# The steps ahead of the first routed tiles of a two-layer gated cross-attention kernel: moved between engines, cut into small steps and put in a written list

## The chip, the cores and the metric

The kernel runs on one core of a Trainium2 chip, as one launch. The time is that of the device in microseconds, the median of several runs. The core's engines work side by side, each through its own queue of instructions in order: TensorE (PE: matmuls into PSUM), VectorE (DVE), ScalarE (ACT), GpSimd (POOL), and SyncE (SP), which issues most of the transfers; GpSimd issues those with indices. They wait for each other through semaphores. A profile is one execution recorded by the hardware.

## The reference

Everything is float32; 4 batches of 512 tokens, 512 wide, so 2048 tokens in 16 tiles of 128. Two layers, each a gated attention and a gated mixture of experts:

```python
x = x + tanh(g_xattn[0]) * set_attention(layernorm(x), ctx, desc_router, W_q, b_q, itok)
x = x + tanh(g_ffn[0])   * moe32(layernorm(x), ...)     # 32 experts of 256, 6 per token, at most 192 tokens each, and a shared one
x = x + tanh(g_xattn[1]) * causal_mha(layernorm(x), ctx, ctx)
x = x + tanh(g_ffn[1])   * moe8(layernorm(x), ...)      # 8 experts of 352, 2 per token, and a shared one of 704
```

The parts that the change touches are those before the first layer's experts:

```python
# set_attention: 64 sets, each token allows 4 of them (itok), the best 2 are mixed
scores = einsum(layernorm(x) @ W_q.T + b_q, desc_router) / sqrt(512)
scores = where(mask, scores, -inf); top 2; softmax over the two
out = weights @ ctx                                   # per batch, 64 x 512
# moe32's router
scores = sqrt(softplus(h @ gate_w.T)); top 6 of scores + bias
weights = scores of the 6, divided by their sum, times 1.5
pos = running count of the expert's tokens in token order; kept if pos < 192
```

## The kernel before

The x of all 16 tiles stays in SBUF (`xs`). Tile t belongs to batch t // 4; group g (`GROUPS[g]`) is the tiles g, g+4, g+8, g+12, one of each batch. `lnT[g]` holds a group transposed (512 features by 512 tokens); at the start it is the plain x, loaded transposed, later the normalised one.

Up to the first routed tile (`before`, L270 to L711) the orders of TensorE, VectorE and ScalarE are as the program writes them (`manual_schedule`); GpSimd's and SyncE's are left to the scheduler. The work there:

- **Masks** (L293 to L301): for each of the 4 token blocks, VectorE compares the 64 set numbers with the 4 allowed ones (16 instructions), and makes the bias `bm`.
- **Scores' matrix** (L304 to L334): descT times W_q, its mean taken out (`msum`, `mrow`), transposed (`pmt`, `mT`). ScalarE and VectorE each have a part in it, in their queues behind the masks.
- **look1(u)** (L348): mean and variance of x of a part, by two VectorE instructions for a tile. The parts are group 0, group 1, and groups 2 and 3 together.
- **score1(p)** (L357): scores of two groups at once (`pss`), copied by ScalarE and transposed back (`pst`).
- **pick1(u)** (L372): the variance's rsqrt by arithmetic on VectorE (`rsqrt`), scaled and masked scores, the best two (`top_picks`), an exponential by a polynomial on VectorE (`exp_parts`), the weights `wa`.
- **mix1(u)** (L407): the weights transposed (`pw`, `wT`), times ctx; VectorE adds to x with the row sum, ScalarE squares for the next variance.
- **norm2, turn2(p)** (L458, L465): rsqrt, then eight normalised rows `h` on VectorE, each stored to `h_dram` and transposed into `lnT` (TensorE, copied by ScalarE).
- **logits2, gate2(p)** (L476, L502): router scores; gate2 is five steps, almost all on VectorE over 128x256 elements: an exponential, a log, a square root, the six best, the weights.
- **shared0(g, ..., early)** (L570): the shared expert of groups 0 and 1, as work for TensorE beside it.
- **counts** (L649 to L708): running counts of each expert's tokens (`rows2`, `upto`), totals `ptot`, counts `pcnt` to `cnt_dram`, positions `ppos`; from them `look2`, which tells which row of counts to fetch for a slot, and the keys from which each token's six slots are sorted.

Then GpSimd gathers counts (`find0`) and rows (`get0`), and 48 routed tiles of 128 slots run, two matmul groups each (`up0`, `down0`), each result stored to `y_dram`.

Between the layers (L895 to L1381) generators are advanced one step at a time by the list `ORDER`: `s` sums one gathered row of experts' results into x (76 of them, GpSimd gathers `NYK` = 7 ahead; the tiles in the order `FIRST`, `FETCH[t]` rows for a tile), `e2`, `e3` the first layer's shared expert of groups 2 and 3, `n`, `t`, `l` norm, transposition and router scores of a group, `q`, `a` the second attention, `r` the routing, `d` the second layer's shared expert, `k` and `w` loads, `p` the plan of the routed tiles.

The driver of the first part is a hand-written sequence of calls, with generators run to their ends or by `next`.

Of the kernel before, what the change touches and what calls it, by code (L numbers as in the profile page):

```python
# [9 lines left out]
F32 = mybir.dt.float32  # L10
I32 = mybir.dt.int32
AF = mybir.ActivationFunctionType
ALU = mybir.AluOpType
# [4 lines left out]
P = 128  # L18
# [26 lines left out]

ORDER = """
e2 k e2 s e2*2 s*4 e2*2 s*4 e3 s k s e3 s e2 s e2 s*6 n2 e3*2 s*2 e3 s e3 n2*2 t2 s e3 n2*2 s e3 s t2*3 l2 s*8
d2 s*3 d2 l2*2 q s*2 d2 s d2 a0 s d2*2 s*2 a0 a1 s a0 d2*2 s*4 d2 a0*2 d2 s*2 a0 s k a1 s*7 n0*4 s t0*2 n0
t0*2 a1 l0 s l0 s*2 d0 l0 s r0 a1 s*3 d0 a1*2 n3 s r0 d0*2 s*2 d0 n3*3 s r0 n3 s d0 r0 s d0 t3 d0 t3 s*5 n1
t3*2 r0*4 n1 d0 n1*3 l3 t1*4 l3 l1*2 l3 d3 r0 l1 d0 r1 p r1*3 d3*2 r1 d3*3 r1*4 p d3 p*2 w d1 d3 w d1 p d3*2  # L50
d1*3 p*2 d1*4 p d1
# [25 lines left out]
def flamingo_gated(  # L77
# [217 lines left out]
    for g in range(TB):  # L295
        V.tensor_scalar(mask[:, g, :], iota_f, itok_f[:, g, 0:1], None, ALU.is_equal)
        for k in range(1, KSET):
            V.scalar_tensor_tensor(
                mask[:, g, :], iota_f, itok_f[:, g, k : k + 1], mask[:, g, :], ALU.is_equal, ALU.max
            )  # L300
# [44 lines left out]
    def tiles1(u):  # L345
        return [t for g in PARTS[u] for t in GROUPS[g]]

    def look1(u):  # L348

        n = len(tiles1(u))  # L350
        s6 = sm12.tile([P, n, 6], F32, name=f"s61_{u}", tag="s61")
        mv = stats1[u] = sm12.tile([P, n, 2], F32, name=f"mv1_{u}", tag=f"mv1_{u}")
        for j, t in enumerate(tiles1(u)):
            V.bn_stats(s6[:, j, :], xs[t])
            V.bn_aggr(mv[:, j, :], s6[:, j, :])

    def score1(p):  # L357

        pss = ps.tile([P, S], F32, name=f"pss{p}", tag="g")
        for c in range(DC):  # L360
            for a in range(2):
                PE.matmul(
                    pss[a * N : (a + 1) * N, :], lhsT=mT[:, c, :], rhs=lnT[2 * p + a][:, c, :],
                    start=(c == 0), stop=(c == DC - 1),
                )
        sT = work.tile([P, S], F32, name=f"sT{p}", tag="sg")
        A.copy(sT, pss)
        scores1[p] = ps_t.tile([P, B, 2 * N], F32, name=f"pst{p}", tag="pt")
        for k in range(B):
            PE.transpose(scores1[p][:, k, :], sT[:, k * P : (k + 1) * P], ident)  # L370

    def pick1(u):  # L372
# [3 lines left out]
        a = sm12.tile([P, 5, n], F32, name=f"a1_{u}", tag="a1", bufs=2)  # L376
        va, d, m, q, r = [a[:, j, :] for j in range(5)]
        V.tensor_scalar(va, stats1[u][:, :, 1], EPS, None, ALU.add)
# [15 lines left out]
        exp_parts(r, d, m, q)  # L394
# [7 lines left out]
        gates1[u] = d  # L402

# [3 lines left out]
    def mix1(u):  # L407
# [12 lines left out]
        A.copy(wT[:, :na], pw)  # L420

# [31 lines left out]
    def cols(t):  # L453

        g, j = PLACE[t]
        return lnT[g][:, :, j * P : (j + 1) * P]

    def norm2(p):  # L458
        nm, ss, va, nb, _ = [norms2[p][:, j, :] for j in range(5)]
        V.tensor_scalar(va, ss, 1.0 / D, EPS, ALU.mult, ALU.add)  # L460
        rs = rsqrt(va, NP, f"b{p}")
        V.tensor_tensor(nb, nm, rs, ALU.mult)
        norms2[p] = rs, nb

    def turn2(p):  # L465

        rs, nb = norms2[p]
        for j, t in enumerate(tiles2(p)):
            h = work.tile([P, D], F32, name=f"h{t}", tag="row", bufs=NROW)
            V.tensor_scalar(h, xs[t], rs[:, j : j + 1], nb[:, j : j + 1], ALU.mult, ALU.add)  # L470
            nc.sync.dma_start(out=h_dram[t * P : (t + 1) * P, :D], in_=h)
            transposed(cols(t), h, f"pth{t}")
# [3 lines left out]
    def logits2(p):  # L476
        pl = ps.tile([P, S], F32, name=f"pl{p}", tag="u")
        for c in range(DC):
            for a in range(2):
                PE.matmul(  # L480
                    pl[a * E0 : (a + 1) * E0, :], lhsT=gate0_sb[:, c, :], rhs=lnT[2 * p + a][:, c, :],
                    start=(c == 0), stop=(c == DC - 1),
                )
        lT = work.tile([P, S], F32, name=f"lT{p}", tag="sg")
# [5 lines left out]
        A.copy(lgs[p], plt.rearrange("p k e -> p (k e)"))  # L490

# [9 lines left out]
    def gate2(p):  # L501
# [49 lines left out]
        for a in range(2):  # L551
            nc.sync.dma_start(out=hd[:, :, 2 * p + a, D:], in_=wts[:, :, a, :])

# [15 lines left out]
    def shared0(g, wgu, wd, early):  # L569

        it = work.tile([P, I0 // P, S], F32, name=f"it0s_{g}", tag="it")
        for ic in range(I0 // P):
# [8 lines left out]
            if not early:  # L581
                yield
# [25 lines left out]

# [3 lines left out]

    ws0 = load_w0(0, wsgu0, wsd0)
    mix = [mix1(u) for u in range(len(PARTS))]
    score1(0)
    look1(0)
    run(pick1(0))
    look1(1)
    next(mix[0])
    next(mix[0])  # L620
    score1(1)
    run(pick1(1))
    look1(2)
    next(mix[1])
    next(mix[1])
    pick = pick1(2)
    next(pick)
    norm2(0)
    turn2(0)
    run(pick)  # L630
    logits2(0)
    for _ in range(2):
        next(mix[2])
        next(mix[2])
    route0, route1 = gate2(0), gate2(1)
    early0, early1 = [shared0(g, *ws0, True) for g in range(EARLY)]
    next(early0)
    next(route0)
    norm2(1)
    next(early0)  # L640
    turn2(1)
    run(route0)
    logits2(1)
    run(early0)
    next(early1)
    next(early1)
    for _ in range(4):
        next(route1)
# [6 lines left out]
    V.tensor_tensor(row_sum, rows2[:, :, 3, :], sel2[:, :, 3, :], ALU.add)  # L655
    for k in range(B):
        V.tensor_tensor(upto[:, k + 1, :], upto[:, k, :], row_sum[:, k, :], ALU.add)
    V.tensor_tensor(rows2, rows2, upto[:, :B, None, :].to_broadcast([P, B, TB, E0]), ALU.add)
    ptot = ps.tile([P, NT, E0], F32, name="ptot", tag="g")
    prior = rows2.rearrange("p k j e -> p (k j) e")  # L660
    PE.matmul(ptot[:, : NT - 1, :], lhsT=ones, rhs=prior[:, 1:, :], start=True, stop=True)
    PE.matmul(ptot[:, NT - 1, :], lhsT=ones, rhs=upto[:, B, :], start=True, stop=True)
    run(route1)
    pcnt = ps.tile([P, B, P], F32, name="pcnt", tag="u")
    for k in range(B):
        PE.matmul(pcnt[:, k, :], lhsT=sel2[:, k, :, :], rhs=tri1, start=True, stop=False)
        PE.matmul(pcnt[:, k, :], lhsT=rows2[:, k, :, :], rhs=ones, start=False, stop=True)
    counts = work.tile([P, B, P], F32, name="counts", tag="row", bufs=NROW)
    A.copy(counts, pcnt)
    nc.sync.dma_start(out=cnt_dram[: NT * E0, :].rearrange("(k p) t -> p k t", p=P), in_=counts)  # L670
    ppos = ps.tile([P, NT, E0], F32, name="ppos", tag="o")
    PE.matmul(ppos, lhsT=tri, rhs=sel2.rearrange("p k j e -> p (k j) e"), start=True, stop=False)
    PE.matmul(ppos, lhsT=ones, rhs=prior, start=False, stop=True)

    ended = flat[:, : NT * E0]
    in_tile = sm12.tile([P, 2, E0], F32, name="in_tile")
    for h in range(2):
        V.tensor_scalar(ended, ptot.rearrange("p t e -> p (t e)"), slot_no[:, 0, h : h + 1], None, ALU.is_le)
        V.tensor_reduce(in_tile[:, h, :], ended.rearrange("p (t e) -> p e t", e=E0), AX.X, ALU.add)
    lookf = sm12.tile([P, NQ, 3], F32, name="lookf")  # L680
    for r, h, s_, p_ in ((0, 0, 0, slice(0, P)), (2, 0, 1, slice(0, P)), (1, 1, 0, slice(0, HC)), (1, 1, 1, slice(HC, P))):
        V.scalar_tensor_tensor(
            lookf[p_, :, r], in_tile[p_, h, s_::2], float(E0), expert[p_, :, r], ALU.mult, ALU.add
        )
    look2 = const.tile([P, NT2], I32, name="look2")
    V.tensor_copy(look2, lookf.rearrange("p q r -> p (q r)"))
    tok2 = const.tile([P, NT2], F32, name="tok2")
    V.scalar_tensor_tensor(
        tok2, lookf.rearrange("p q r -> p (q r)"), float(P // E0), neg4e.rearrange("p q r -> p (q r)"),
        ALU.mult, ALU.add,  # L690
    )
# [7 lines left out]
    back_, zrow_ = [  # L699
        v.rearrange("p q s -> p (q s)")[:, None, :].to_broadcast([P, NT, E0]) for v in (back, zrow)  # L700
    ]
    V.scalar_tensor_tensor(key2, ppos, float(P), back_, ALU.is_ge, ALU.mult)
    V.tensor_tensor(key2, key2, ppos, ALU.subtract)
    V.scalar_tensor_tensor(
        kept2, ppos, float(CAP), sel2.rearrange("p k j e -> p (k j) e"), ALU.is_lt, ALU.mult
    )
    V.tensor_tensor(key2, key2, zrow_, ALU.add)
    V.tensor_tensor(key2, key2, kept2, ALU.mult)  # L708
    run(early1)
# [197 lines left out]
    FIRST = [6, 2, 14, 10, 3, 11, 15, 7, 0, 4, 8, 12, 5, 1, 9, 13]  # L907
# [468 lines left out]
    for what in ORDER.split():  # L1376
        what, _, n = what.partition("*")
        for _ in range(int(n or 1)):
            next(does[what])
    for steps in does.values():  # L1380
        assert next(steps, None) is None  # L1381
# [233 lines left out]
```

## Time and profile before

| | us |
|---|---|
| median of 3 runs (lowest, highest) | 1103.65 (1103.22, 1107.76) |
| the profiled execution | 1109.61 |
| its span, first to last instruction | 1107.9 |

Busy time of the engines by stage of the profiled execution, in us, and the clock granted to TensorE (1 is full):

| stage | from, to | PE | DVE | ACT | POOL | clock |
|---|---|---|---|---|---|---|
| first scores and picks | 0, 33 | 15.9 | 20.8 | 3.7 | 6.4 | 0.71 |
| second and third part | 33, 62 | 11.0 | 26.6 | 6.7 | 0 | 0.68 |
| rows, logits, first gating | 62, 110 | 44.8 | 42.1 | 21.6 | 4.3 | 0.93 |
| second gating, counts | 110, 156 | 38.1 | 36.3 | 7.9 | 12.7 | 0.93 |
| routed tiles | 156, 456 | 298.0 | 92.9 | 64.0 | 91.5 | 1.00 |
| between the layers | 456, 700 | 202.7 | 141.7 | 61.8 | 131.1 | 0.78 to 0.93 in its parts |
| routed tiles of layer 2 and the end | 700, 1108 | 396.7 | 105.8 | 45.3 | 130.3 | 0.98 to 1.00 |

How to read what follows: a row of a timeline gives start, duration, engine, line, operation, output<-input, shape and count; in brackets the idle time before it and what ended that. A row of the windows gives the stretch, its length, the busy time of PE, PE's weight loads, DVE, ACT and POOL (with counts), the granted clock, the DMA engines' share and GB/s.

### The profile page before, as it was taken

The numbers are of one execution on the slowest core, as the hardware profiler recorded it, in microseconds if no ns is written. First come the engines' busy times: TensorE is split into PE (matmuls) and PEld (weight loads), VectorE is DVE, ScalarE is ACT, GpSimd is POOL, SyncE is SP. The second block draws the span as 40 slices with busy tenths as digits, with TensorE's granted clock in tenths as the row PEclk, the third lists the DMA queues.
The fourth block names the chain that finished last, engine by engine and source line by source line (L and its number), as shares of the span: only waits on it lengthen the run. The fifth ranks groups of instructions, "written<-read, shape, count | busy, mean of one in ns | idle before, by whom it ended". The sixth has DMA issues, their size and how long they took to land. (4 is left out here: it accounts for less than half of the span.)

```text
span 1107.9 us, 11070 instructions
## 1 busy us (share of the span) xinstructions
PE 1007.1 (91%) x3334; PEld 492.9 (44%) x3334; DVE 466.1 (42%) x1244; ACT 210.9 (19%) x461; POOL 376.3 (34%) x413
## 2 busy tenths in 40 slices
PE   5479889999999999969779896999999998999998
PEld 2134444444444444424434443655555555544443
DVE  5989946322222232357787443122222222218111
ACT  1144121222222222123343200211111111110000
POOL 2001142234332222276552562445545454310000
PEclk7679999999999999989969798999999999999999
DMA  8522047688788787765563107527453744438111
GB/s 320 234 76 77 11 125 238 222 275 283 257 294 287 253 288 248 252 204 172 145 206 115 48 5 207 184 74 238 133 163 107 248 115 145 135 117 313 38 38 38
DMA packets 88477, 191.94 MB, mean 173 GB/s; under 512 B 24638, under 2 KB 42078, under 8 KB 82016
## 3 DMA queue, kind: packets, MB, share of 16 engines
q1 hardware_dynamic: 59808, 114.59, 29.3%
q0 software_dynamic: 28608, 76.63, 23.4%
q8 instruction: 27, 0.44, 0.2%
q14 instruction: 34, 0.28, 0.1%
HBM read 206.16 MB, written 35.57 MB: 218 GB/s over the span
## 5 line engine op out<-in xcount | busy, mean ns | idle before, releaser
L801 PE MATMUL gu<-wbuf,xbT 128*128 128x512 f32 (+1 forms) x512 | 174.0, 596 | 1.7 <-ACT xbT L257 0.8
L967 POOL DMA_INDIRECT yk<-y_dram,rows_of x76 | 84.1, 1107 | 89.1 <-DMA kb<-in_kblk_dram 34.7
L783 POOL DMA_INDIRECT xb<-h_dram,get x48 | 48.1, 1002 | 165.5 <-issue 97.3
L1436 PE MATMUL pgr<-wbuf,xrT 128*128 128x352 f32 x288 | 93.2, 467 | 7.4 <-DMA wbuf<-in_wgu_dram,wrow 6.7
L1456 PE MATMUL por<-wbuf,itr 128*128 128x512 f32 (+1 forms) x216 | 98.7, 592 | 0.0
L801 PEld LDWEIGHTS gu<-wbuf,xbT 128*128 128x128 f32 (+1 forms) x512 | 63.1, 163 | 78.7 <-issue 77.3
L808 DVE SCALAR_TENSOR_TENSOR sgb<-gu,xb,sgb 128x256 f32<-128x256 f32 (+1 forms) x64 | 30.9, 483 | 157.6 <-ACT sgb L806 131.8
L1439 DVE SCALAR_TENSOR_TENSOR sgr<-pur,slots,sgr 128x352 f32<-128x352 f32 x36 | 21.0, 584 | 170.0 <-PE pur L1436 105.1
L826 PE MATMUL pob<-wbuf,itb 128*128 128x512 f32 (+1 forms) x256 | 91.2, 599 | 0.0
L1436 PE MATMUL pur<-wbuf,xrT 128*128 128x352 f32 x288 | 91.1, 459 | 0.0
L1227 PE MATMUL pg<-lnT,wbuf 128*128 128x512 f32 (+1 forms) x224 | 85.3, 560 | 0.1
L1459 POOL DMA_INDIRECT y_dram<-yr,put x36 | 36.9, 1025 | 126.5 <-DVE yr L1458 113.6
L1227 PE MATMUL pu<-lnT,wbuf 128*128 128x512 f32 (+1 forms) x224 | 79.5, 531 | 0.0
L1436 PEld LDWEIGHTS pur<-wbuf,xrT 128*128 128x128 f32 x288 | 54.7, 190 | 30.5
L1436 PEld LDWEIGHTS pgr<-wbuf,xrT 128*128 128x128 f32 x288 | 52.7, 193 | 32.1 <-issue 4.5
L1243 PE MATMUL po<-wbuf,it 128*128 128x512 f32 x128 | 61.2, 612 | 3.0 <-DVE x L1253 3.0
L1456 PEld LDWEIGHTS por<-wbuf,itr 128*128 128x128 f32 (+1 forms) x216 | 41.0, 190 | 41.9 <-issue 34.9
L761 POOL DMA_INDIRECT found<-cnt_dram,look x48 | 48.7, 1014 | 25.9 <-issue 14.0
L1227 PEld LDWEIGHTS pg<-lnT,wbuf 128*128 128x128 f32 (+1 forms) x224 | 35.6, 183 | 43.8 <-issue 42.0
L1227 PEld LDWEIGHTS pu<-lnT,wbuf 128*128 128x128 f32 (+1 forms) x224 | 35.0, 175 | 40.8 <-issue 38.1
L831 DVE COPY y<-pob 128x512 f32<-128x512 f32 x48 | 33.2, 692 | 45.3 <-PE pob L826 32.0
L1458 DVE TENSOR_TENSOR yr<-por,half_db 128x512 f32<-128x512 f32 x36 | 24.9, 692 | 57.5 <-PE por L1456 51.2
(398 smaller groups left out, 1279.2 us busy)
## 6 DMA issues: line engine op xcount, KB each, us to landing
wbuf<-in_wgu_dram SPq DMA_DIRECT2D x32, 1024.0 KB
wbuf<-in_wd_dram SPq DMA_DIRECT2D x32, 512.0 KB
y_dram<-y SPq DMA_DIRECT2D x48, 256.0 KB
q<-rp SPq DMA_DIRECT2D x256, 32.0 KB
y<-y_dram SPq DMA_DIRECT2D x32, 256.0 KB
lnT<-in_xT_dram SPq DMA_DIRECT2D x4, 1024.0 KB
x<-in_x_dram SPq DMA_DIRECT2D x16, 256.0 KB
h_dram<-h SPq DMA_DIRECT2D x16, 256.0 KB
```

The source lines that it names most:

```text
L761: G.indirect_dma_start(out=found[k][:, j, :], out_offset=None, in_=cnt_dram[:, :], in_offset=bass.IndirectOffsetOnAxis(ap=look2[:, i : i + ...
L783: G.indirect_dma_start(out=rows0[i], out_offset=None, in_=h_dram[:, :], in_offset=bass.IndirectOffsetOnAxis(ap=get2[:, i : i + 1], axis=0) ...
L801: PE.matmul(gu[p_, :], lhsT=xbT[:, c, p_], rhs=weights[e][0][:, c, :], start=(c == 0), stop=(c == DC - 1),)
L808: V.scalar_tensor_tensor(sg[p_, :I0], gu[p_, I0:], xb[p_, D + e : D + e + 1], sg[p_, :I0], ALU.mult, ALU.mult)
L826: PE.matmul(po[p_, :], lhsT=it[:, ic, p_], rhs=weights[e][1][:, ic, :], start=(ic == 0), stop=(ic == I0 // P - 1),)
L831: V.tensor_copy(y, po)
L967: G.indirect_dma_start(out=yk, out_offset=None, in_=y_dram[:, :], in_offset=bass.IndirectOffsetOnAxis(ap=rows_of[:, t, k : k + 1], axis=0) ...
L1227: PE.matmul(p_[m, :n], lhsT=wgu[:, a, c, i], rhs=lnT[g][:, c, k], start=(c == 0), stop=(c == DC - 1))
L1243: PE.matmul(po, lhsT=it[:, ic, k * P : (k + 1) * P], rhs=wd[:, ic, :] if ic < 2 else wd2, start=(ic == 0), stop=(ic == 2),)
L1436: PE.matmul(p_, lhsT=xbT[:, c, :], rhs=wgu[:, a, c, :], start=(c == 0), stop=(c == DC - 1))
L1456: PE.matmul(po, lhsT=it[:ni, ic, :], rhs=wd[:ni, ic, :], start=(ic == 0), stop=(ic == 2))
L1459: d = G.indirect_dma_start(out=y4_dram[:, :], out_offset=bass.IndirectOffsetOnAxis(ap=put4[:, i : i + 1], axis=0), in_=yr, in_offset=None, ...
```

## The change

The masks are formed on GpSimd by differences and products, with one compare on VectorE. look1 takes the mean by matmuls of the transposed x with a column of ones, and the squared deviations by ScalarE. pick1's exponential is ScalarE's. The normalised rows `h` are ScalarE's, in a step of their own apart from the transposition. score1, pick1, mix1, norm2, logits2, gate2 and the early shared0 get more step ends (`yield`). The counts become a generator. A new helper `in_steps` advances generators by a list, and the first part is driven by `FIRST_ORDER`; `j` in it is a matmul whose result nobody reads. `ORDER` is another list of the same steps, and `FIRST` another order of the tiles within each group.

```diff
+FIRST_ORDER = """
+c0 c1 c0*2 c1 c0*2 b0*2 f0 c1 f0*2 c1*2 f1 m0*3 f1 j c2*2 b1 f1 c2 m1*2 b1 c2*3 m1 c2*2 n0 c2 h0*4 t0 h0 t0 h0
+f2 t0 f2*2 t0*2 m2 h0*2 m2*3 t0*3 g0 m2 n1 h1*2 e0 g0 t1 h1*2 e0*2 h1 e0 t1 h1 r0*2 t1 h1 t1 e0 r0 t1 h1 t1*3
+g1*2 r0*2 r1*4 o e0 e1 e0 e1*2 e0 o*3 r1 e1*2 j o e1*2 o e1 o
+"""
 ORDER = """
-e2 k e2 s e2*2 s*4 e2*2 s*4 e3 s k s e3 s e2 s e2 s*6 n2 e3*2 s*2 e3 s e3 n2*2 t2 s e3 n2*2 s e3 s t2*3 l2 s*8
-d2 s*3 d2 l2*2 q s*2 d2 s d2 a0 s d2*2 s*2 a0 a1 s a0 d2*2 s*4 d2 a0*2 d2 s*2 a0 s k a1 s*7 n0*4 s t0*2 n0
-t0*2 a1 l0 s l0 s*2 d0 l0 s r0 a1 s*3 d0 a1*2 n3 s r0 d0*2 s*2 d0 n3*3 s r0 n3 s d0 r0 s d0 t3 d0 t3 s*5 n1
-t3*2 r0*4 n1 d0 n1*3 l3 t1*4 l3 l1*2 l3 d3 r0 l1 d0 r1 p r1*3 d3*2 r1 d3*3 r1*4 p d3 p*2 w d1 d3 w d1 p d3*2
-d1*3 p*2 d1*4 p d1
+e2 s e2*3 s*2 k e2 s*3 k s e2*2 s*2 e2 s*2 e3 s*4 e3 s*3 n2 e3*2 n2*2 s*4 n2 e3 t2 s t2 n2 e3 s t2 s t2 e3*2
+s*5 d2 s*6 d2 l2 q s*3 d2 a0 s l2 s*2 l2 s*3 d2 s d2*2 a0 s*2 a1 a0 s d2*2 s a0 s*2 d2 a0 k a1 s*5 d2 n0 s
+n0*4 t0*4 a0 l0 s a1 s*5 a1 l0 s l0 d0 s a1 d0*2 a1 n3 d0 r0 n3 s r0 n3 r0 d0 n3 d0 s*2 n3 t3 d0 t3 s t3 s*2
+t3 l3 d0 s*4 n1 r0 n1*2 r0 d0 l3 r0 n1*2 d3 t1*2 l3 t1*2 l1*3 r1*2 r0*2 d1 r1*2 d3 r1 r0 r1 d0 p r1 p*3 d1 w
+d3*2 p d1 d3 d1 d3*3 r1 d1 d3 d1 d3 w r1 p*2 d1*2 p d1*2
 """
...
-    for g in range(TB):
-        V.tensor_scalar(mask[:, g, :], iota_f, itok_f[:, g, 0:1], None, ALU.is_equal)
-        for k in range(1, KSET):
-            V.scalar_tensor_tensor(
-                mask[:, g, :], iota_f, itok_f[:, g, k : k + 1], mask[:, g, :], ALU.is_equal, ALU.max
-            )
+    hit = chain[:, 1:5, :].rearrange("p a n -> p (a n)").rearrange("p (k g n) -> p k g n", k=KSET, n=N)
+
+    for k in range(KSET):
+        G.tensor_tensor(
+            hit[:, k], iota_f[:, None, :].to_broadcast([P, TB, N]),
+            itok_f[:, :, k : k + 1].to_broadcast([P, TB, N]), ALU.subtract,
+        )
+    G.tensor_tensor(hit[:, 0:2], hit[:, 0:2], hit[:, 2:4], ALU.mult)
+    G.tensor_tensor(mask, hit[:, 0], hit[:, 1], ALU.mult)
+    V.tensor_scalar(mask, mask, 0.0, None, ALU.is_equal)
     V.tensor_scalar(bm, mask, 1.0, BIG, ALU.subtract, ALU.mult)
...
     def look1(u):
 
-        n = len(tiles1(u))
-        s6 = sm12.tile([P, n, 6], F32, name=f"s61_{u}", tag="s61")
-        mv = stats1[u] = sm12.tile([P, n, 2], F32, name=f"mv1_{u}", tag=f"mv1_{u}")
-        for j, t in enumerate(tiles1(u)):
-            V.bn_stats(s6[:, j, :], xs[t])
-            V.bn_aggr(mv[:, j, :], s6[:, j, :])
+        ts = tiles1(u)
+        st = stats1[u] = sm12.tile([P, 2, len(ts)], F32, name=f"st1_{u}")
+        px = ps.tile([P, len(ts)], F32, name=f"px{u}", tag="u")
+        for j, t in enumerate(ts):
+            for c in range(DC):
+                PE.matmul(px[:, j : j + 1], lhsT=cols(t)[:, c, :], rhs=ones[:, 0:1], start=(c == 0), stop=(c == DC - 1))
+        V.tensor_scalar(st[:, 0, :], px, -1.0 / D, None, ALU.mult)
+        yield
+        for j, t in enumerate(ts):
+            x_ = work.tile([P, D], F32, name=f"xa{t}", tag="xn")
+            A.activation(x_, xs[t], AF.Square, bias=st[:, 0, j : j + 1], accum_out=st[:, 1, j : j + 1])
+            yield
...
         V.tensor_tensor(d, v[:, :, 1], v[:, :, 0], ALU.subtract)
-        exp_parts(r, d, m, q)
+        V.tensor_scalar(d, d, -87.0, None, ALU.max)
+        A.activation(r, d, AF.Exp)
+        yield
         V.tensor_scalar(d, r, 1.0, None, ALU.add)
...
-    def turn2(p):
+        yield
+
+    hs = {}
+
+    def rows2_(p):
 
         rs, nb = norms2[p]
         for j, t in enumerate(tiles2(p)):
-            h = work.tile([P, D], F32, name=f"h{t}", tag="row", bufs=NROW)
-            V.tensor_scalar(h, xs[t], rs[:, j : j + 1], nb[:, j : j + 1], ALU.mult, ALU.add)
+            h = hs[t] = work.tile([P, D], F32, name=f"h{t}", tag="row", bufs=NROW)
+            A.activation(h, xs[t], AF.Identity, bias=nb[:, j : j + 1], scale=rs[:, j : j + 1])
             nc.sync.dma_start(out=h_dram[t * P : (t + 1) * P, :D], in_=h)
-            transposed(cols(t), h, f"pth{t}")
+            yield
+
+    def turn2(p):
+
+        for t in tiles2(p):
+            transposed(cols(t), hs.pop(t), f"pth{t}")
+            yield
...
-            if not early:
-                yield
+            yield
...
+    def filler():
+
+        while True:
+            pj = ps_t.tile([P, DC, P], F32, name="pj", tag="pt")
+            PE.matmul(pj.rearrange("p c t -> p (c t)"), lhsT=ones, rhs=ctx_sb[:, 0, :], start=True, stop=True)
+            yield
+
+    def in_steps(order, does):
+        does = does | {"j": filler()}
+        for what in order.split():
+            what, _, n = what.partition("*")
+            for _ in range(int(n or 1)):
+                next(does[what])
+        for what, steps in does.items():
+            assert what == "j" or next(steps, None) is None
...
+    ws0 = load_w0(0, wsgu0, wsd0)
+    does = {"o": count2()}
+    for p in range(2):
+        does |= {f"b{p}": score1(p), f"n{p}": norm2(p), f"h{p}": rows2_(p), f"t{p}": turn2(p), f"g{p}": logits2(p)}
+        does |= {f"r{p}": gate2(p), f"e{p}": shared0(p, *ws0, True)}
+    for u in range(len(PARTS)):
+        does |= {f"c{u}": look1(u), f"f{u}": pick1(u), f"m{u}": mix1(u)}
+    in_steps(FIRST_ORDER, does)
...
-    FIRST = [6, 2, 14, 10, 3, 11, 15, 7, 0, 4, 8, 12, 5, 1, 9, 13]
+    FIRST = [2, 10, 14, 6, 7, 15, 3, 11, 0, 8, 4, 12, 9, 5, 1, 13]
```

`count2` (`o`) holds the lines of the counts as they were, in seven steps: row sums; totals `ptot`; counts with their copy and store; positions `ppos`; `in_tile`; `look2`; keys. In the steps of the other generators: `b` is matmuls, then copy and transposes; `f` ends before top_picks, after the Exp, and after `wa`; `m` begins with a step of its own for `pw` and `wT`; `g` is matmuls, then the rest; `e` has eight steps (gate and up matmuls, then ScalarE's and GpSimd's part, twice; four output tiles).

## The prediction

> **What bounds the kernel now.** I read, in this order, the page's slices, the engine timelines of the first 160 us, the granted clock in stretches of 1 us, and the timelines between the layers. The slices first (40 of 27.7 us, busy tenths):
>
> ```profile
> PE   5479889999999999969779896999999998999998
> DVE  5989946322222232357787443122222222218111
> PEclk7679999999999999989969798999999999999999
> ```
>
> From slice 7 on TensorE is full except around slices 17 to 24. Both places where it is not full are those of the change. Whatever the head loses or gains is passed on one to one, because 156 to 456 us is a solid block of matmuls (298 of 300 us busy). Inside the head, DVE sets the time:
>
> ```profile
> 82.57 0.42 DVE L505 SCALAR_TENSOR_TENSOR chain<-lg 128x256 f32<-128x256 f32 x1
> ...
> 133.54 0.68 DVE L658 TENSOR_TENSOR rows<-rows,upto 128x512 f32<-128x512 f32 x1
> ```
>
> Between these two lines DVE hardly stops: gate2 of both halves and the row sums, 51.6 us, of which 7.3 (88.2 to 95.5) are the second norm2 and eight rows. So 44.3 us of gating follow r0's first instruction. Then comes a tail of latency: ptot at 134.37, gathers, first routed transpose at 154.64. **The question is when r0 can start,** with the other 7.3 us counted to it.
>
> **The parts, priced.**
>
> *Masks.* Removed from DVE: 4 times (0.25 + 0.93), 6.91 to 11.53 us. Added on GpSimd, whose rows are 0.44 us for 128x128 (L166) and 1.29 for 128x512 (L587), so about 0.7 for 128x256: 4 x 0.7 + 1.3 + 0.7 = 4.8 us after itok_f at 6.9, thus 11.7. The compare (0.3) stands in DVE's queue ahead of bm, msum, mrow and bq_desc, which TensorE waits for: msum at 12.3 instead of 11.74, +0.6 (bounds -0.5 and +3: broadcasts free, or twice as dear). pmt then ends at 15.7.
>
> *Means.* The 16 bn pairs leave DVE: 16 x 0.80 = 12.8 us. In come 64 f32 matmuls of a 128x128 weight with one moving column. The nearest row has the same weight and 8 columns, four matmuls a line, warm and cold:
>
> ```profile
> 517.85 0.95 PE L1028 MATMUL plt<-fold,lT 128*128 128x8 f32 x8
> ...
> 616.06 1.87 PE L1028 MATMUL plt<-fold,lT 128*128 128x8 f32 x8
> ```
>
> So a tile of means costs 0.95 us at full clock and 1.87 at half; the weight load sets it, so one column is no cheaper. Which clock? pmt and pss before show it:
>
> ```profile
> 12.55 1.94 PE L327 MATMUL pmt<-ident,mrow 128*128 128x64 f32 x8 [4.04 <-DVE bq_desc L324]
> ...
> 15.57 6.26 PE L362 MATMUL pss<-lnT,mT 128*64 128x512 f32 x16 [0.46 <-ACT mT L330]
> ```
>
> The clock falls to 0.50 at 10.8, while TensorE waits, and is not back until about 20.9, though TensorE was busy from 12.55 but for half a microsecond. The other place:
>
> ```profile
> 616.00:617.00 1.00, 1.00 (x7) 0.94 (x5) 0.00 (x0) 0.59 (x2) 0.69 (x2) 0.50 0.15 5
> 617.00:618.00 1.00, 1.00 (x9) 0.98 (x12) 0.03 (x1) 0.00 (x0) 0.70 (x2) 0.50 0.08 3
> ...
> 627.00:628.00 1.00, 1.00 (x2) 0.43 (x2) 0.42 (x1) 0.00 (x0) 0.79 (x1) 0.50 0.12 16
> 628.00:629.00 1.00, 1.00 (x3) 0.30 (x2) 0.00 (x0) 0.00 (x0) 0.19 (x1) 0.78 0.02 1
> ```
>
> The last number but two is the clock. TensorE is nearly always busy from 614.5 (small transposes, 8-column matmuls), yet only after six more microseconds of 512-column matmuls does it rise. The Trainium skill, "TensorE: Matmul & The Clock Gate" (Part 1: The HAM clock gate), says that the clock doubles after some 3.4 us of sustained activity. By the rule the first eight tiles cost 3.4 + 6.2 x 0.95 = 9.3 us; by the rows, where few columns do not count as activity, 8 x 1.87 = 15.0. I take the row, for the first eight and, less 1.5 for the chance that the filler leaves the clock up for a while, 13.5 for the last eight (bounds 7.6 and 15.0).
>
> *Squares.* 16 x 0.70 (pitch of L440) = 11.2 us on ScalarE, mostly idle there, but each waits for a mean.
>
> *Exponentials.* 26.12 to 28.71 on DVE, 2.6 us, three times; in come a maximum (0.2) and a 128x4 activation (0.2, row L143) with two hand-overs (0.1): 2.1 gained each time. Page "ScalarE: Activation LUTs" (Table sets: the hidden batching unit) puts exp and tanh into one set, and a switch at 2.7 us with its drain; the trace has one load in the head, 0.81 to 2.09, with Tanh running on it, and a switch at L584 at 1.28. By the shared set nothing is added; if another set was loaded, 1.28 by the row, and idle time hides it, since the load does not wait for the data. I take 0.
>
> *Rows.* 3.74 us on DVE for eight, twice; on ScalarE 2.92 for four (L1009 at 596.45), so 5.8 for eight. DVE gains 7.5, but h now needs ScalarE, with the squares and PSUM copies.
>
> The eight stores of rows to h_dram go with them on SP's queue, where nothing is left to pass (its weight loads are issued by 34 us), and are read only from 151 on: 0.
>
> *Removed from DVE in all:* about 4.3 + 12.8 + 6.3 + 7.5 = 31 us. Before r0 DVE has 71 us to do (64 until 82.57, and the 7.3), so 40 remain. If DVE stayed the bound, r0 would start far earlier. It does not stay the bound.
>
> **The walk along FIRST_ORDER.** "c0 c1 ... b0": TensorE does the means of two groups ahead of the scores. 15.7, px0 to 23.2, px1 to 30.7, pss (cold, 6.3) to 37.0, sT and pst to 38.4. Before, the scores were there at 23.2: **+15.2**. What covers this on DVE? Nothing but one rsqrt (2.2). f0 then takes 0.9 + 1.8 + 0.4 + 0.3 + 0.6 + 1.3 = 5.3: wa at 43.7 (before 30.6). pw, wT 1.3, four cold sums 3.3, filler 0.9: 49.2. px2 13.5: 62.7. Here the new wait bites: st2 = px2 times -1/D stands in DVE's queue ahead of f1's last third, so wa1, and with it m1, waits; TensorE has pss1 next anyway (6.3): 69.0. pw1, wT 1.1, sums 3.3, squares 3.0: 76.4. n0 2.2: 78.6. f2: rsqrt and scores 3.6, picks 3.4, exp 0.5, wa 2.7: 88.8 (before 73.3). pw2, wT 1.3; eight sums, cold at first, 7.4: 97.5. ScalarE has three PSUM copies ahead of the last four squares: 102.4; n1 to 104.6. TensorE meanwhile: last turns 99.5, pl0 4.1, then e0's gate and up matmuls (7.2), listed ahead of plt, which ends 111.3; lg at 111.8: **r0 starts at 111.8**. Against 82.6 + 7.3 = 89.9 that is **+22**. From there 44.3 us of DVE as before. Second half: rows, turns, e0's other 7.2 us, its first po and g1 put lg1 at about 135, r1 needs it at 133: +0 to +2. e1's 14.4 us of matmuls end near 156, as the row sums do. The tail is unchanged; e1's last ScalarE and GpSimd steps now follow the counts, which the 10 us up to the gathers hide. Head: +22, bounds +12 and +28.
>
> **The list between the layers.** The work is the same; only waits can go. The biggest of TensorE's:
>
> ```profile
> 487.80 1.02 PE L598 MATMUL po0s<-wbuf,it0s 128*128 128x512 f32 x2
> 498.92 4.43 PE L598 MATMUL po0s<-wbuf,it0s 128*128 128x512 f32 x6 [10.09 <-DVE it0s L591]
> ```
>
> GpSimd issues a yk gather every 1.33 us, landing 4 us later; 18 sums must precede n2. In the new list all of e2 and 15 sums lie ahead of e3's second step; walking it with these paces, e3's second it0s comes at 492.5 with TensorE done at 490.4: a wait of 2. By 504 some 30 of the 76 sums are done instead of 23, seven times 1.33 = 9 us ahead. After that DVE (attention, sums) is close to the bound, and the end (scatters, table, 7.94 us wait at pslot) is listed much the same. FIRST only reorders the four tiles inside each group. The first k step (the shared expert's weights, on SP's queue) is listed later, behind three sums and four steps of e2, and TensorE needs it first at d2, some 30 us on: 0. I take -10; bounds -20 and +6, since stops whose cause the trace does not name (DVE 5.1, 3.6, 10.3 us; ScalarE 29.1 in three) can fall elsewhere.
>
> **Sum:** +22 - 10 = +12 on the profiled execution, 1109.61 us (span 1107.9): 1121.6. That execution lies 6.0 above the median of the runs, 1103.65; on the median the sum is **1116 us**.
>
> **Rivals.**
> (a) *The clock does rise on the means* (or the means cost less): one mechanism, px at 0.24 us a matmul instead of 0.47. Place: 15.7 to 63 us. Price: 7.4 + 5.9 us of px and some 5 of cold pss behind them, so +22 becomes about +4, and with the list -10: 1098. With the first px warm as well, head -3: 1091. It decides once the mean of a tile is below about 1.2 us. For it: the rule; against it: 614 to 628 and 12.6 to 20.9 us. Chance 0.22, centre 1096.
> (b) *The list between the layers gains nothing* (sums wait for the it0s as before, unnamed stops move into the path), and masks are dear: 1103.65 + 24 + 2 = 1130. For it: those stops; against it: the walk up to 504. Chance 0.18.
> (c) The forecast, 0.60, own range 1106 to 1126.
>
> About 0.5% (5.5 us) is what this measurement tells from no change. Slower: 0.52 of (c), all of (b), 0.01 of (a): 0.71. Same: 0.06 + 0.04: 0.10. Faster: 0.02 + 0.17: 0.19. The range 1094 to 1132 leaves out the warmer half of (a) and the end of (b).
>
> **What would show it.** px0 and px1 at 7.5 us each at clock 0.50; pst near 38; DVE idle over half of the first 110 us; r0's first instruction near 112; first routed transpose near 177 (154.64 + 22). The sums between the layers: 30 by 54 us after the last routed pg0s starts (450.4 before), and no 10 us wait at po0s. Wrong it would be if px runs at 0.95 a tile, or if r0 starts before 90.

## The result: slower, by more than twice the forecast

| | before | after |
|---|---|---|
| median of four runs, us (lowest, highest) | 1105.7 (1103.22, 1108.89) | 1134.34 (1132.72, 1136.82) |
| ratio, 95% interval | | 1.026 (1.022 to 1.0299) |
| span of the profiled execution | 1107.9 | 1131.0 |

The forecast was 1116, with a range up to 1132. The sign was right, the size was not: +28.6 us instead of +12. Three rows of the page of after (TensorE, VectorE and TensorE's clock, in 40 slices of 28.3 us) show the first quarter changed and the dip at slices 18 to 24 still there:

```profile
PE   6758989999999999997779895999999898999998
DVE  1454974422232223166687551222222222218111
PEclk7668999999999999999889897999999999999999
```

DVE, which was at 5, 9, 8, 9, 9 tenths in the first slices, is now at 1, 4, 5, 4, 9: it was relieved, and waits. VectorE's timeline of after gives the two ends of the gating (start, duration, then in brackets the idle time and what ended it):

```profile
109.28 0.43 DVE L541 SCALAR_TENSOR_TENSOR chain<-lg 128x256 f32<-128x256 f32 x1 [6.50 <-ACT lg L525]
...
154.04 0.69 DVE L686 TENSOR_TENSOR rows<-rows,upto 128x512 f32<-128x512 f32 x1
```

44.8 us lie between them, as forecast (44.3). r0 was forecast at 111.8 and comes at 109.3; the row sums start at 154.0 where they started at 133.5. TensorE's timeline of after shows why:

```profile
14.25 1.94 PE L340 MATMUL pmt<-ident,mrow 128*128 128x64 f32 x8 [4.34 <-DVE bq_desc L337]
...
16.73 13.81 PE L373 MATMUL px<-ones,lnT 128*128 128x1 f32 x64
30.48 5.12 PE L386 MATMUL pss<-lnT,mT 128*64 128x512 f32 x16
...
48.01 11.38 PE L373 MATMUL px<-ones,lnT 128*128 128x1 f32 x64
```

The scores (`pss`), which began at 15.6, begin at 30.5, behind the means of eight tiles (64 records, two a matmul). The first routed matmul comes at 175.4 instead of 156.0: the head costs **19.4 us**, near the +22 of the forecast.

Of the 23.1 us between the two spans, 18.8 have accrued where the first shared expert of the next stage starts, 3.6 are added between the layers (from there to the first transposition of layer 2's routed tiles), 0.7 after it. The rest of the 28.6 is that before's profiled execution (1109.61) lay 3.9 above the median of its runs, and after's (1132.72) 1.6 below. The list between the layers was to give 10 us. It gave nothing. That is what the experiments are about, beside the means.

### The profile page after: what moved, and what is told of

Same layout as the page of the kernel before. It is cut to its first block, busy times and chain, and to the rows that moved or that the text cites. A ratio compares the mean times of both kernels' runs of the same rounds, so it can differ in the third digit from the quotient of the medians.

```text
span 1131.0 us, 11301 instructions
## 1 busy us (share of the span) xinstructions
PE 1033.7 (91%) x3466; PEld 517.2 (46%) x3466; DVE 437.4 (39%) x1148; ACT 233.3 (21%) x512; POOL 381.7 (34%) x419
## 3 DMA queue, kind: packets, MB, share of 16 engines
q1 hardware_dynamic: 59808, 114.59, 28.6%
## 5 line engine op out<-in xcount | busy, mean ns | idle before, releaser
L841 DVE SCALAR_TENSOR_TENSOR sgb<-gu,xb,sgb 128x256 f32<-128x256 f32 (+1 forms) x64 | 30.9, 483 | 157.0 <-ACT sgb L839 131.3
L1464 PEld LDWEIGHTS pur<-wbuf,xrT 128*128 128x128 f32 x288 | 54.7, 190 | 30.5
L1276 PE MATMUL po<-wbuf,it 128*128 128x512 f32 x128 | 64.8, 642 | 3.9 <-DVE x L1286 3.9
L623 POOL TENSOR_TENSOR it0s<-it0s,sg0s 128x512 f32<-128x512 f32 x4 | 5.3, 1330 | 140.7 <-ACT it0s L622 140.7
```

The costliest lines, as they stand in the source:

```text
L841: V.scalar_tensor_tensor(sg[p_, :I0], gu[p_, I0:], xb[p_, D + e : D + e + 1], sg[p_, :I0], ALU.mult, ALU.mult)
L1276: PE.matmul(po, lhsT=it[:, ic, k * P : (k + 1) * P], rhs=wd[:, ic, :] if ic < 2 else wd2, start=(ic == 0), stop=(ic == 2),)
L1464: PE.matmul(p_, lhsT=xbT[:, c, :], rhs=wgu[:, a, c, :], start=(c == 0), stop=(c == DC - 1))
```

## The experiments

A ratio is always to the kernel before on the same chip. The runs came in three sets, on three chips: head, list, w late and means; the second time of after, the two combined versions and the fillers; the third time of after, before's second trace and the last row. The first measurement stands apart from them. The table has starts in us from the traces, one trace for each row. "Scatter", "table" and "ptr" are the last slot scatter, the issue of the table's read (`tab`) and layer 2's first routed transposition, counted from the first e2 matmul, so that the head drops out.

| run | ratio (95%) | r0 | first routed matmul | scatter | table | ptr |
|---|---|---|---|---|---|---|
| before | 1 | 82.6 | 156.0 | 209.5 | 220.8 | 241.0 |
| before, second trace | 1.0005 (0.9987 to 1.0022) | 82.7 | 157.7 | 202.0 | 212.9 | 234.9 |
| after | 1.026 (1.022 to 1.0299) | 109.3 | 175.4 | 221.0 | 229.1 | 244.6 |
| after, second time | 1.0118 (1.0086 to 1.0149) | 109.4 | 175.5 | 210.1 | 218.5 | 233.0 |
| after, third time | 1.0169 (1.0139 to 1.0198) | 109.0 | 176.1 | 207.5 | 215.8 | 231.7 |
| head alone | 1.0166 (1.0112 to 1.0219) | 110.6 | 177.8 | 201.2 | 211.3 | 232.5 |
| list alone | 0.9971 (0.9955 to 0.9988) | 82.5 | 156.1 | 211.3 | 219.7 | 235.5 |
| after, w late | 1.0100 (1.0063 to 1.0136) | 109.2 | 176.3 | 196.2 | 207.6 | 228.7 |
| after, means on VectorE | 1.0014 (0.9995 to 1.0033) | 90.0 | 157.0 | 208.0 | 215.5 | 231.5 |
| the last two together | 0.9919 (0.9887 to 0.9951) | 92.3 | 158.3 | 191.0 | 201.2 | 221.7 |
| the same, g0 earlier | 0.9939 (0.9917 to 0.9962) | 88.0 | 159.9 | 190.2 | 200.4 | 220.1 |
| after, fillers | 1.0266 (1.0229 to 1.0304) | 122.5 | 188.6 | 207.5 | 214.8 | 229.5 |
| before, list, w late | 0.9895 (0.9868 to 0.9922) | 81.7 | 155.3 | 192.9 | 202.9 | 223.1 |

**1. The two halves apart.** The head alone, and the list alone:

```diff
 # head alone: the changed kernel
-ORDER, FIRST as changed
+ORDER, FIRST as before
 # list alone: the kernel before
-ORDER, FIRST as before
+ORDER, FIRST as changed
```

> The changed kernel with the lists of before (ORDER and FIRST): the head's change alone. My theory (head +19.4, as the first routed tile shows, list about +4 because of its weight gathers): 1124 to 1127, some 6 below the changed kernel. Rival, that the list gives its -10 and the head costs more than the profile of one execution shows (nearly +38): 1140 or more, above the changed kernel. Rival, that the list's loss is larger than one profile shows (+9): 1122.

> The kernel before with ORDER and FIRST of the change: the list alone. My theory: +3 to +9, 1108 to 1114, with the wait at po0s near 3 instead of 10 and the last slot scatter some 11 us later from the stage's start. The prediction's term was -10, which would give 1095. Rival, that the list suits only the changed head: clearly more than +9.

Head alone: 1121.94 us, +17.9 on the median, while its trace has r0 20.7 us late (110.6 against 82.6 + 7.3) and the first routed matmul 21.8: the theory of a head near +19 stands within the interval (+12 to +24), though the median lies below what I expected. List alone: 1101.72, about -3 by the ratio (its interval, -1 to -5); the +3 to +9 that I expected from the first trace was wrong as well as the -10. The scatter did come late, 211.3 against 201.2 and 202.0 with the old list. So the list's gain and its loss nearly cancel.

**2. The w steps.** In the new list the two steps `w` (GpSimd gathers of a routed tile's weights) stand ahead of the last eight and the last four scatters of r1; in the old one behind all of them.

```diff
-... r1 p r1 p*3 d1 w
-d3*2 p d1 d3 d1 d3*3 r1 d1 d3 d1 d3 w r1 p*2 d1*2 p d1*2
+... r1 p r1 p*3 d1
+d3*2 p d1 d3 d1 d3*3 r1 d1 d3 d1 d3 r1 w*2 p*2 d1*2 p d1*2
```

> The changed kernel, both w steps (the gathers of two routed tiles' weights, 17 KB a row) listed after the last r1 instead of ahead of its last eight and last four scatters. My theory: the last scatter no longer stands behind 4.5 MB of weights on GpSimd's queue, goes at some 205 us from the stage's start instead of 221, and the table is read 8 to 10 us earlier: 1124 to 1127, 7 to 10 below the changed kernel. Rival, that DVE's routing steps, listed late among d1 and d3, set the last scatter, and the weights only fill a gap: within 3 of the changed kernel. Rival, that the weights' own arrival sets the first routed tile: slower than the changed kernel by a few us.

GpSimd's timeline of after shows the place:

```profile
665.48 1.05 POOL L1295 DMA_INDIRECT wbuf<-in_wgu_dram,wrow  x1 [0.30 <-DVE tile_f L1353]
666.83 1.01 POOL L1295 DMA_INDIRECT wbuf<-in_wd_dram,wrow  x1 [0.30 <-issue]
668.15 1.03 POOL L1125 DMA_INDIRECT slot_dram<-ent,slot  x1 [0.30 <-issue]
...
674.34 1.05 POOL L1295 DMA_INDIRECT wbuf<-in_wgu_dram,wrow  x1 [0.30 <-issue]
675.70 1.01 POOL L1295 DMA_INDIRECT wbuf<-in_wd_dram,wrow  x1 [0.30 <-issue]
679.85 1.03 POOL L1125 DMA_INDIRECT slot_dram<-ent,slot  x1 [3.14 <-DMA wbuf<-in_wgu_dram,wrow]
681.77 1.01 POOL L1125 DMA_INDIRECT slot_dram<-ent,slot  x1 [0.89 <-DMA wbuf<-in_wd_dram,wrow]
688.91 0.98 POOL L1125 DMA_INDIRECT slot_dram<-ent,slot  x1 [6.13 <-DMA slot_dram<-ent,slot]
690.20 0.98 POOL L1125 DMA_INDIRECT slot_dram<-ent,slot  x1 [0.30 <-issue]
```

A scatter moves eight bytes for each partition, a w step 17 KB. The scatters at 679.85 and 681.77 wait for the weights issued at 665.48 and 666.83, each the eighth transfer before it; the one at 688.91 waits for the scatter issued at 668.15, which took over 20 us to land behind those weights. Only then is the table read (SyncE's timeline, and TensorE's wait for it):

```profile
698.29 0.33 SPq L1358 DMA_DIRECT2D tab<-slot_dram  x1
```

```profile
700.45 1.05 PE L1361 MATMUL pslot<-pick,tab 128*128 128x39 f32 x4 [12.63 <-DMA tab<-slot_dram]
```

With w late the last scatter came at 196.2 of the stage instead of 210.1 and 207.5 in the second and third trace of after, and ptr 4.3 and 3.0 us earlier. On the whole 1115.74, a ratio of 1.0100. Against the three measurements of after (1.0118 to 1.026) this is in the right direction, but the lowest of them lies inside its interval, so with the changed head as it is the gain is shown by the traces only. With the head of before, and with the means back on VectorE, it is shown by the times too (experiment 5: 0.9971 becomes 0.9895, and 1.0014 becomes 0.9919, the intervals apart each time).

**3. The means.** VectorE's two instructions a tile in the place of matmuls and squares:

```diff
-        px = ps.tile([P, len(ts)], F32, name=f"px{u}", tag="u")
...
-        V.tensor_scalar(st[:, 0, :], px, -1.0 / D, None, ALU.mult)
         yield
         for j, t in enumerate(ts):
-            A.activation(x_, xs[t], AF.Square, bias=st[:, 0, j : j + 1], accum_out=st[:, 1, j : j + 1])
+            V.bn_stats(s6[:, j, :], xs[t])
+            V.bn_aggr(mv[:, j, :], s6[:, j, :])
             yield
```

> The changed kernel with look1's mean and variance by two VectorE instructions a tile again, in the places where the list has the squares (each pair in one step of c); masks, exponentials, rows and both lists as changed. My theory: 25 us of cold one-column matmuls leave TensorE's path, DVE takes 12.8 us back into its idle time: r0 starts 15 to 25 us earlier, the whole is 1110 to 1119. Rival, that the rows and squares on ScalarE or the order of the list set r0, and the means lie beside them: 1130 or more. Rival, that DVE becomes the bound again: 1125.

1104.55 us, below all that I expected; the ratio is 1.0014. VectorE's timeline of this run:

```profile
89.96 0.43 DVE L539 SCALAR_TENSOR_TENSOR chain<-lg 128x256 f32<-128x256 f32 x1 [6.52 <-ACT lg L523]
```

r0 is 19.3 us earlier than in after, the first routed matmul 18.4: **in the traces the means on TensorE are all but one microsecond of the head's loss.** And the rest of the head's change brings nothing: r0 is where the kernel before would have it with its second norm and rows done (82.6 + 7.3 = 89.9), though exponentials, rows and masks have left VectorE. It waits 6.5 us for `lg`.

The times put the means somewhat lower. The second and third measurement of after lie 0.0104 and 0.0155 above this run, 11 to 17 us. And this run lies 0.0043, nearly 5 us, above the list alone, which ran in the same set with the head of before; their intervals (0.9995 to 1.0033 and 0.9955 to 0.9988) do not touch. So the head's other moves, in the places that this list gives them, cost some microseconds rather than nothing; single traces, which differ by as much from one execution to the next, do not show where. A list made for means on VectorE was not tried.

**4. The clock.** One 128x512 matmul, which nobody reads, behind each tile's four:

```diff
                 PE.matmul(px[:, j : j + 1], lhsT=cols(t)[:, c, :], rhs=ones[:, 0:1], ...)
+            pj = ps_t.tile([P, DC, P], F32, name=f"pk{t}", tag="pt")
+            PE.matmul(pj..., lhsT=ones, rhs=lnT[PLACE[t][0]][:, 0, :], start=True, stop=True)
```

> The changed kernel with one 128x512 matmul (like j) behind each tile's four one-column matmuls, 16 in all. Theory C, that the clock follows the columns streamed and one-column matmuls count as idle: the granted clock rises to 1.00 within some 6 us of px's start, a tile with its filler takes 1.4 warm, px0 and px1 together 14 to 16 us, pss 3.7 instead of 5.1; the whole within 4 us of the changed kernel. Rival D, that the clock follows something else (load of the chip, the weights' loads): it stays at 0.50 through px, each filler adds 0.95 us: px0 and px1 21 us, the whole 12 to 15 us slower than the changed kernel.

1132.82 us, 16.3 above the changed kernel in the same set; the head was 13.2 us later than in after. Neither theory had it whole. The windows of this run (length, busy PE, weight loads, DVE, ACT, POOL, then the granted clock, the DMA engines' share, GB/s) show a cold stretch and a warm one with the same mix of work:

```profile
24.00:26.00 2.00, 2.00 (x6) 1.39 (x6) 0.00 (x0) 0.00 (x0) 0.00 (x0) 0.50 0.99 416
...
66.00:68.00 2.00, 2.00 (x12) 1.33 (x11) 0.00 (x0) 0.00 (x0) 0.00 (x0) 1.00 0.00 0
```

TensorE's timeline has, from start to start, 1.57 us for a tile's means and 1.85 for the filler in the first, 0.81 and 0.94 in the second:

```profile
26.42 1.71 PE L373 MATMUL px<-ones,lnT 128*128 128x1 f32 x8
27.99 2.05 PE L375 MATMUL pk<-lnT,ones 128*128 128x512 f32 x2
29.84 0.42 PE L373 MATMUL px<-ones,lnT 128*128 128x1 f32 x2
...
66.29 0.95 PE L373 MATMUL px<-ones,lnT 128*128 128x1 f32 x8
67.10 1.10 PE L375 MATMUL pk<-lnT,ones 128*128 128x512 f32 x2
68.04 0.95 PE L373 MATMUL px<-ones,lnT 128*128 128x1 f32 x8
```

Started cold, 27 us of this mix never raised the clock; pss, all 512 columns, did within 4 us. Started warm, behind four sums and j, it held the clock at 1.00 for all 14 us. In after, without fillers, the means lost it (the same columns):

```profile
48.00:50.00 2.00, 2.00 (x20) 2.00 (x19) 1.90 (x14) 1.22 (x3) 0.00 (x0) 1.00 0.00 0
50.00:52.00 2.00, 2.00 (x14) 2.00 (x14) 0.63 (x5) 1.81 (x7) 0.00 (x0) 0.63 0.00 0
52.00:54.00 2.00, 2.00 (x11) 2.00 (x11) 0.00 (x0) 0.00 (x0) 0.00 (x0) 0.50 0.00 0
```

TensorE is 100% busy in all three lines, and its clock falls from full to half. That is theory C for the fall; for the rise theory C is too simple, since the columns of the filler did not suffice. The load of the DMA engines, which also differs between the two stretches (0.99 and 0.00), is not the reason: in after `pss` raised the clock between 32 and 36 us (0.63, then 1.00) with a DMA share of 1.08 and 0.95, and the fall at 50 us came with a share of 0.00.

**5. Versions that beat both, and what the head's other moves are worth.** Means on VectorE with w late; the same with g0's second step ahead of e0's first (`h1*2 e0 g0` to `h1*2 g0 e0`); and the kernel before, its head untouched, with the new list and w late.

```diff
 # g0 earlier
-m2 n1 h1*2 e0 g0 t1 h1*2 e0*2
+m2 n1 h1*2 g0 e0 t1 h1*2 e0*2
 # before, list, w late
-ORDER, FIRST as before
+ORDER, FIRST as changed, with the edit of experiment 2
```

> Means by VectorE again and both w steps after the last r1. With means on VectorE alone the table's read is issued at 664.6, 7.5 us after the last slot scatter, which stood behind the weights. My theory: the last scatter at some 647 to 650, the table 5 to 8 us earlier: ratio 0.994 to 0.997 to the kernel before. Rival, that the weights now come later than the first routed tile needs them, or that routing sets the last scatter: 1.000 to 1.003.

> As the one before, and g0's second step (lT, plt, lg) listed ahead of e0's first (7.1 us of matmuls). In the kernel with means on VectorE, VectorE waits 6.52 us for lg at 89.96. My theory, by the prediction's step that e0's matmuls ahead of plt delay r0 by their whole length: r0 at 83 to 85, first routed tile 5 to 6 us earlier, ratio 0.989 to 0.992. Rival, that r0 is not on the path (lg1 or the second half sets the counts): within 1 us of the one before.

> The kernel before with ORDER and FIRST of the change and both w steps after the last r1; its head untouched. With the w where the change has them the list alone gave 0.9971, and moving them gave 3.5 to 10 us behind the changed head. My theory, that the head's other moves (rows, exponentials, masks off VectorE) brought nothing, since its first routed tile (158.3) is no earlier than before's (156.0): 0.988 to 0.993, equal to or better than the version with means on VectorE (0.9919). Rival, that those moves do help: 0.995 or more.

1094.6, 1094.57 and **1091.25 us**. The last has the lowest ratio, 0.9895, though its interval overlaps those of the first two. Against the list alone, with w where the change put it (0.9971), its last scatter and ptr are 18.5 and 12.4 us earlier in the stage. So the new list is worth some 12 us, of which the two w steps took about 8 back. Its head is before's, and its first routed matmul (155.3) is not later than in the versions with the changed one: the moves off VectorE bought no time. GpSimd's and SyncE's timelines of the best version show the end of the stage as it should be, the last scatter, then the weights, the table's read 10 us behind the scatter:

```profile
641.81 0.98 POOL L1092 DMA_INDIRECT slot_dram<-ent,slot  x1 [0.30 <-DMA slot_dram<-ent,slot]
643.10 1.05 POOL L1262 DMA_INDIRECT wbuf<-in_wgu_dram,wrow  x1 [0.30 <-issue]
```

```profile
651.87 0.33 SPq L1325 DMA_DIRECT2D tab<-slot_dram  x1
```

The g0 step lost its bet. Of VectorE in that run:

```profile
88.05 0.43 DVE L539 SCALAR_TENSOR_TENSOR chain<-lg 128x256 f32<-128x256 f32 x1 [3.25 <-ACT lg L523]
118.24 0.42 DVE L539 SCALAR_TENSOR_TENSOR chain<-lg 128x256 f32<-128x256 f32 x1 [7.30 <-ACT lg L523]
```

r0 starts 4.2 us earlier, but TensorE stood idle for lT, its clock fell, e0's matmuls moved behind, and r1 waits 7.3 us for the second half's `lg`; `ptot` is 3.2 us later than without. TensorE waits little between the two, so what was put behind `lg` delays the second half.

**6. Both kernels again.**

> The changed kernel once more, beside the others. Head alone gave a ratio of 1.0166 and the list alone 0.9971, which add to 1.0137, against 1.026 measured for both. Theory A, that the two parts add and the first measurement of both held stops of up to 4 us on VectorE and ScalarE that no semaphore explains (marked remote in its trace, none in the four later ones): 1.012 to 1.016, 1117 to 1121. Theory B, that the list costs more behind the changed head: 1.022 to 1.030 again, and the remote stops are back.

> The changed kernel a third time. The first measurement gave 1.026 with stops in its trace that no semaphore explains between the layers (ptr 244.6 us behind the first e2), the second 1.0118 with none (233.0). Theory A, that the stops belong to the run's place and not to the kernel: near 1.012 where the trace has none, near 1.026 where it has them. Theory B, that they belong to the kernel and come and go from execution to execution: times of both kinds within one set of runs, 1114 to 1137.

> The kernel before, for its trace: its first profile has 48 us of unexplained stops on VectorE and ScalarE and 241.0 us from the first e2 to ptr; with the same list behind the changed head that stretch took 232.5. If the stops are not the kernel's: none here, 231 to 234 us, and the whole near 1100. If they are: 240 again.

1116.54, then 1121.93, each with six runs close together (1114.77 to 1118.56, 1118.32 to 1123.51), where the first measurement had four between 1132.72 and 1136.82. The product of head and list alone, 1.0137, lies between the two repeats. So 10 to 15 us of the first 28.6 (28.6 less 18.4 and 13.5) were not seen again. The traces say where they sit: the stage between the layers took 244.6 us in the first and 233.0 and 231.7 in the repeats. In after's first trace ScalarE and VectorE stop there for nothing that a semaphore in the record explains. The page calls most such waits "remote"; the second one here it puts down to TensorE, whose matmuls had long ended:

```profile
525.72 1.29 DVE L641 TENSOR_TENSOR x<-po0s,x 128x512 f32<-128x512 f32 x2 [3.50 <-remote]
```

```profile
545.09 0.67 ACT L1265 ACTIVATE sg<-pg,gb_sb 128x512 f32<-128x512 f32 x1
555.64 0.48 ACT L1265 ACTIVATE sg<-pg,gb_sb 128x256 f32<-128x256 f32 x1 [9.89 <-PE pq L1197]
```

The matmuls for the second activation ended at 547.7 in that trace, 8 us before it; in the repeat it starts 0.1 us behind them, at 544.28. TensorE itself paused four times in those 8 us, 0.35 to 0.98 us between its next matmuls, for nothing that the profile shows. Laid beside the second trace, TensorE's work in the stage is 3.5 us ahead before the first stop and 0.9 behind after it, 1.9 behind before the second and 8.4 after it, and 11.6 at the stage's end.

A wait without a named releaser is not by itself a stop, though. Before's first trace has three on ScalarE, 29.1 us in all, which the prediction names among the unexplained; in its second trace the same three instructions wait 27.9 us, and two of them have a named releaser. What differs there is VectorE: its waits of 5.1, 3.6 and 10.3 us become none, 2.0 and 4.7, and the stage takes 234.9 us instead of 241.0.

This fits theory A of the two repeats, that the stops do not belong to the kernel: times and traces go together, set by set. It is no more than that, since each set has one trace of after and the sets ran on different chips. What causes the stops was not found. The records show no code load in the 3.5 us of the first one, and in the second one only a load that the repeat has at the same place; no run was made that could bring the stops about.

## Why the prediction was right in the head and wrong in the list

- **Masks:** right. Subtractions took 0.62 us, products 1.26 and 0.72. From `itok_f` to `msum` it is 6.05 us instead of 5.25: +0.8, forecast +0.6. (itok itself arrived 0.9 later, in before's second trace 0.7 later.)
- **Means:** right. 1.72 us a tile cold (forecast 1.87), 13.8 for the first eight (15.0), 11.4 for the last (13.5). The clock stayed at 0.50 throughout the first eight, as the rows argued. The rule that the prediction cites from the Trainium skill, "TensorE: Matmul & The Clock Gate" (Part 1: The HAM clock gate), full clock after some 3.4 us of sustained activity, would have made them 9.3; with one-column matmuls it did not hold here, though TensorE was busy for all 13.8 us.
- **Exponentials and rows:** right in themselves. VectorE waited 0.27 us for an Exp, and no table load was added for it. But their gain was counted as VectorE's only, and it was hidden, as the walk had it.
- **The walk:** right. pst's scores at 37.0 (38.4), VectorE's wait for px2 with f1 behind it 8.76 us, wa2 at 85.6 (88.8), r0 at 109.3 (111.8), the tail +20.5 at ptot and +19.4 at the first routed matmul. +22 was measured as +19.4.
- **The list between the layers: "I take -10". This is the step that failed.** It stood on three readings. The first took po0s' wait of 10.09 us as the list's. About half of it is a stop with no releaser (5.08 us on VectorE, which the prediction had itself named among the unexplained); TensorE's timeline of before's second trace and of after has

```profile
496.06 5.23 PE L598 MATMUL po0s<-wbuf,it0s 128*128 128x512 f32 x6 [4.68 <-DVE it0s L591]
```

```profile
512.68 1.12 PE L634 MATMUL po0s<-wbuf,it0s 128*128 128x512 f32 x2 [2.84 <-DVE it0s L627]
```

  so the wait fell as forecast (to 2.8, forecast 2), but from 4.7. The second was that by 54 us of the stage 30 of the 76 sums would be done instead of 23, which is 9 us. Counted on VectorE's timelines it was 25 (25 and 29 in the repeats, 26 with the list alone), against 25 and 27 with the old list outside the first trace. A lead came later, where the prediction counted none: the 50th sum starts at 86 to 89 us of the stage (98.1 in after's first trace) against 99.1 and 100.4. The third was that "the end (scatters, table, 7.94 us wait at pslot) is listed much the same". It is not: the walk stopped at 504 us and did not follow the w steps, which were moved past r1 on GpSimd's queue. In traces other than the first two, the first scatter did go 2 to 8 us earlier (144.9 to 150.0 of the stage, against 152.0 and 153.3 with the old list), and the last one, with w as changed, went 5 to 10 later (207.5 to 211.3 against 201.2 and 202.0). The net is -3 us (list alone), +3.6 in the recorded trace. A gain of the predicted size was in the list, as experiment 5 shows, but not where the walk had put it.
- **The sum:** +22 - 10 = +12 against 28.6. Of the 16.6 between them the list is 13.6 (-10 against +3.6), the head -3.2 (18.8 where the next stage starts), the end 0.7. The other 5.5 is the step from one execution to the median: the prediction let after lie below its profiled execution as before did, by 6.0, while before lay 3.9 below with the fourth run, and after 1.6 above. Most of the list's 13.6, 11.6 to 12.9 us, is not in the same kernel's repeats, whose 1116.5 and 1121.9 lie near the forecast. That is no credit to the step: it reached them with a head too dear and a list too good.
- **Rivals:** (a) fell with the clock. (b), 1130, came nearest; its list part, stops included, was right for the first measurement, its dear masks were not.

## What to carry to other kernels

When steps of a written list move, walk every queue to the end of the stage, and ask of each large transfer which small one is now issued behind it on the same queue. Work moved to an engine with idle time costs its full length if it is put ahead of the first link of a latency chain, and relief of an engine that only waits on that chain is worth nothing. Before a wait is booked as a gain, see whether a second trace of the same kernel has it at the same size; whether its releaser is named does not settle it.

## What the hardware showed that was not expected

- TensorE, 100% busy by the records with one-column matmuls, lost its full clock within some 3 us and stayed at half for the 9 us that they still ran. With every tile's means followed by a 512-column matmul, the clock was kept for 14 us if it was up, and not raised in 27 us if it was down; `pss`, 512 columns throughout, raised it within 4 us. In these runs the rise asked for more than the hold.
- A small scatter issued on GpSimd's queue behind 2.2 MB of gathered weights took over 20 us to land. In this program each of GpSimd's transfers waits for the one issued eight before it, so the delay passed on to the last scatters; with the weights behind them, the table was read 10 us after the last scatter's issue.
- The same kernel measured 1134.3, 1116.5 and 1121.9 us in three sets of runs, while the kernel before, beside it, stayed between 1103.0 and 1105.7: most of the difference in the first arose in one stage, around stops for which the profile shows no cause. Their cause stays open.
